# Layer 2's forward x transform on rows folded onto their mirror image

## The chip, the cores and the metric

The kernel runs on one core of a Trainium2 chip. The metric is the device time of one execution in microseconds, as the median of several runs. The engines are TensorE (PE, with its weight loads shown as PEld), VectorE (DVE), ScalarE (ACT), GpSimd (POOL), and the DMA queues of SyncE (SP) and POOL.

## The reference

Four layers are applied to x of shape (16, 16, 256, 256) in float32: samples, channels, rows y, columns x. Each normalizes x over groups of two channels, computes something from it and adds that to x. Layer 0 is a 3x3 convolution written with FFTs, layer 1 a diagonal 5-tap convolution, layer 3 a quantized 3x3 convolution. The change touches layer 2 alone:

```python
x = x + _L2_conv_ref(_gn(x), ty, tx, weights_pole1, weights_pole2, weights_residue)

alpha = jnp.fft.fft2(x, axes=(-2, -1))
A = 1.0 / (omega1[:, None, None, None] - weights_pole1[None])
Bm = 1.0 / (omega2[:, None, None, None] - weights_pole2[None])
S = jnp.einsum('ikpq,oikp,xikq->oxik', weights_residue, A, Bm)
output_residue1 = jnp.einsum('biox,oxik->bkox', alpha, S)
C = jnp.einsum('biox,oikp->bikpx', alpha, A)
D = jnp.einsum('bikpx,xikq->bikpq', C, Bm)
output_residue2 = jnp.einsum('bikpq,ikpq->bkpq', D, weights_residue)
x1 = jnp.fft.ifft2(output_residue1, s=(Ny, Nx), axes=(-2, -1)).real
...
return x1 + x2 / Nx / Ny
```

`alpha` is the two-dimensional Fourier transform of each image. `S` mixes channels at each frequency, and `x1` is the inverse transform of the mixed spectrum. `C` and `D` reduce alpha over both frequencies against the poles' responses; they give `x2`.

## The kernel before

The program has five stages, one after the other: layers 0 and 1 (their last matmul starts at 1271 us), the forward transforms of layer 2 (`forth` from 1342 to 2147 us), the mixing of channels at each frequency (to 2920 us), the inverse transforms (2958 to 3806 us), and layer 3 (from 3833 us). The change is in the second stage, in tables that it reads, and in one table of the inverse transform (`last`).

Transforms are matmuls with tables of cosines and sines. The input is real, so only 129 of 256 frequencies in x are kept, `fx`: 128 first, then the even ones (65 columns with 128), then the odd ones (64 columns).

The work of the second stage is ordered by the list `order`: for each block of four samples, for each pair of channels, for each of the four samples. One entry of it is a call of `quarters` (line 763), which prepares the two images of a pair; there are 128. `quarters` loads the images with y on the partitions (`xt`), adds and subtracts the upper and the lower half of y (`u`: the sum with the mean folded in by VectorE at line 768, the difference by GpSimd at line 769), and from `u` makes sums and differences of column w and column w + 128 (`qd`, two operations of VectorE, line 772). The sums carry the even x frequencies, the differences the odd ones. Everything that goes through the helper `tt` has line 191 in the profile.

For each image then come:

- `forth` (from line 775): the transform along y. For each of the two column parities c, `v` (that is `qd`) is the weight matrix of 128 x 128, and the y tables (line 782) and `hats[0]`, the y poles' responses (line 785), stream through, 128 columns each. ScalarE scales the result into `y` (line 787): its partitions are the 128 columns w, its columns 128 real parts, 128 imaginary parts, 128 for the poles.
- `across` (from line 790): the transform along x. `y`'s real and imaginary parts are the weights, in turn; the tables `x1` and `x2` stream through (line 796), 2 x 65 columns for the even frequencies and 2 x 64 for the odd ones, all over 128 rows. ScalarE copies the first part's sums out of PSUM (`pc`, line 801), and two operations of VectorE combine both parts into `al`, for the frequencies fy and -fy (lines 803 and 804). After four samples `al` goes to DRAM in two DMAs, one on SP's queue and one on POOL's (line 807).
- `onto` (from line 810): after four images, the poles' part of `y` is multiplied with `hats[1]`, the x poles' responses, in four parts of the array of 32 columns (line 817). VectorE multiplies the result with the residues (`prod`), GpSimd adds the products up (`acc`).

The order on TensorE is written out by hand: `forth` of one image, then `across` of the image before it, then, once in four images, `onto`. The order on the other engines is a scheduler's, and it is fixed in the program. Between these steps `transforms` and `prepared` work out further tables for this stage and for the next (`hat`, `qe`, `qg`, `qw`, `ps_t`, `af`, `l`).

Buffers: `xt` four, `u` and `qd` three each, `ps_y` three PSUM banks, `ps_a` three (an image takes two), `ps_d` two.

Of the kernel before, what the change touches and what calls it, by code (L numbers as in the profile page):

```python
# [57 lines left out]
P = 128  # L58
C = 16
# [12 lines left out]
def constants():  # L72

    n = np.arange(N)
    m = np.arange(128)
    even, odd = 2 * np.arange(64), 2 * np.arange(64) + 1
    fx = np.concatenate([[128], even, odd])
    fy = np.stack([np.concatenate([even, odd]), -np.concatenate([[128], even[1:], odd])], 1).reshape(-1)

    def cos(a, b):  # L80
        return np.cos(2.0 * np.pi * (np.outer(a, b) % N) / N)

    def sin(a, b):
        return np.sin(2.0 * np.pi * (np.outer(a, b) % N) / N)


    y1 = [np.concatenate([cos(m, even), cos(m, [128]), -sin(m, even[1:])], 1),
          np.concatenate([cos(m, odd), -sin(m, odd)], 1)]
    by_fx = [fx[:65], fx[65:]]
    x1 = [np.concatenate([cos(m, f), -sin(m, f)], 1) for f in by_fx]  # L90
    x2 = [np.concatenate([sin(m, f), cos(m, f)], 1) for f in by_fx]

    full = np.stack([np.stack([cos(o, m), sin(o, m)], 1) for o in (n[0::2], n[1::2])], 1)


    inv = np.stack([np.stack([np.concatenate([cos(even, m), v * cos([128], m), v * sin(even[1:], m)], 0),
                              np.concatenate([cos(odd, m), v * sin(odd, m)], 0)], 1) for v in (-1, 1)], 2)

    h = 0.5 / N**2
    last = np.stack([h * np.concatenate([cos([0], m), 2 * cos(even[1:], m), cos([128], m), -2 * sin(even[1:], m)], 0),  # L100
                     h * np.concatenate([2 * cos(odd, m), -2 * sin(odd, m)], 0)], 1)
    p = np.arange(P)[:, None]
    q = np.arange(P)[None, :]
    c16, c8, c4 = np.arange(C)[None, :], np.arange(8)[None, :], np.arange(S)[None, :]
    s = p % S
    strip = np.stack([s == c4, s + 1 == c4, s - 1 == c4], 1)
    nat = (n + 128) % N - 128


    f4 = p % 4  # L110
    alone = np.concatenate([np.where(f4 < 2, 0.5, 1.0), np.where(f4 < 2, 0.5 - f4, 1.0)], 1)
    im = p // 32 % 2 == 1
    sa = np.where(p < 64, [[1.0, 1.0]], [[1.0, -1.0]])
    sb = np.where(p < 64, [[1.0, -1.0]], [[-1.0, -1.0]])
    parts = {
        "y1": np.concatenate(y1, 1), "x1": np.concatenate(x1, 1), "x2": np.concatenate(x2, 1),
        "full": full, "inv": inv, "last": last, "alone": alone,
        "not0": 1.0 * (p > 0),
        "strip": strip,
        "chan": p % 64 // S == c16,  # L120
        "imag": 1.0 * (p // C % 2 == 1), "real": 1.0 * (p // C % 2 == 0),
        "group4": (p % 32 // 4 == q % 32 // 4) / 16.0,
        "first": p == 4 * c8,
        "mod": p % 8 == c8,


        "turn": np.stack([np.where(p < 64, 1.0, -1.0), np.where(p // 32 % 2 == 0, -1.0, 1.0),
                          1.0 * (p // 32 % 2 == 1), 1.0 * (p // 32 % 2 == 0)], 1),

        "turn_q": np.concatenate([np.where(im, sb, -sa), np.where(im, -sa, -sb)], 1),  # L130
        "vi": 1.0 * ((p // 64 == np.arange(16)[None, :] // 8) & (p % 8 == np.arange(16)[None, :] % 8)),
        "diag": p // NP % 4 == c4,
        "own": p // 32 == c4,
        "m1": np.diag(np.where(p[:, 0] // 16 % 2 == 0, 1.0, -1.0)) / (2 * N) ** 2,
        "m2": (p == q + 16 - q // 16 % 2 * 32) / (2 * N) ** 2,
        "eye": 1.0 * (p == q),
        "mean": np.full((P, P), 1.0 / P),
        "ones": np.ones((P, P)),
        "quarter": np.concatenate([np.where(p // 16 % 2 == 0, 0.25, 0.0), np.where(p < 64, 0.25, 0.0)], 1),
        "sign": np.where(p < 64, 1.0, -1.0),  # L140
        "nat": nat.reshape(128, 2),
    }
    at, where, cols = 0, {}, []
    for k, v in parts.items():
        v = np.asarray(v, np.float32).reshape(P, -1)
        where[k] = (at, v.shape[1])
        at += v.shape[1]
        cols.append(v)
    fxs = np.where(fx == 128, -128, fx)
    rows = np.concatenate([fy, np.where(fy == -128, 128, fy), fxs, fx])  # L150
    return np.concatenate(cols, 1), rows.astype(np.float32)[None, :], where
# [14 lines left out]
def layers(ctx, tc, x, w0, w1, w3, sw, bias, ty, tx, p1a, p1b, p1c, p2a, p2b, p2c, resa, resb,  # L166
# [402 lines left out]
    def sums_over_q(pool, psum):  # L569
# [32 lines left out]
        for h in range(HC):  # L602
            for k0 in range(0, C, KQ):
# [14 lines left out]
                       bc(bc(vi[:, v], 1, 8), 1, 2 * KQ), MUL)  # L618
                yield
                for k in range(KQ):  # L620
                    ps = psum.tile([P, 512], F32, tag="ps_a", name="ps_t")
                    for m in range(2):
                        nc.tensor.matmul(ps[:, m * NX : (m + 1) * NX], start=m == 0, stop=m == 1, rhs=e[:, k],
                                         lhsT=w[:, 2 * k + m].rearrange("p v r i -> p (v r i)"), skip_group_check=True)
                    nc.scalar.copy(t2[:, h, k0 + k].rearrange("p r x -> p (r x)"), ps[:, 0 : 2 * NX])
                    if k % 2:
                        yield

        a = new(pool, [HC, C], "qa")
        Q.tensor_copy(a, t2[:, :, :, 0, 0])  # L630
        Q.tensor_scalar(t2[:, :, :, 0, 0], t2[:, :, :, 1, 0], -1.0, None, MUL)
        Q.tensor_copy(t2[:, :, :, 1, 0], a)
        yield

    afs, lss, sks = {}, {}, {}
    KC = 4
# [40 lines left out]
    with ExitStack() as es:  # L677
        wp = es.enter_context(tc.tile_pool(name="b_w", bufs=1))
        ps_y = es.enter_context(tc.tile_pool(name="b_ps_y", bufs=3, space=PSUM))
        ps_a = es.enter_context(tc.tile_pool(name="b_ps_a", bufs=3, space=PSUM))  # L680
        ps_d = es.enter_context(tc.tile_pool(name="b_ps_d", bufs=2, space=PSUM))

        y1 = table(wp, "y1").rearrange("p (a f) -> p a f", a=2)
        x1, x2 = table(wp, "x1"), table(wp, "x2")
# [9 lines left out]
        ap_ = es.enter_context(tc.tile_pool(name="b_a", bufs=3))  # L694
        with ExitStack() as tmp:
            tp = tmp.enter_context(tc.tile_pool(name="b_t", bufs=1))
            full = table(wp, "full").rearrange("p (h m f) -> p h m f", m=2, h=2)
            nat, diag = table(tp, "nat"), table(tp, "diag")
            ws = []
            for m, t in enumerate((ty, tx)):  # L700
# [6 lines left out]
            def transforms(m, i0, ni, pool):  # L707
# [22 lines left out]
                for o in range(2):  # L730
                    for i in range(0, ni, nb):
                        cols = slice(i * KP, (i + nb) * KP)
                        for r, parts_ in enumerate(((re, im), (im, nre))):
                            ps = ps_y.tile([P, 8, KP], F32, tag="ps_y", name="ps_hat")
                            to = ps[:, 0:nb]
                            for k, v_ in enumerate(parts_):
                                nc.tensor.matmul(to.rearrange("p i k -> p (i k)"), lhsT=full[:, o, k],
                                                 rhs=v_[:, o, cols], start=k == 0, stop=k == 1)
                            hat = hats[m][:, o, i0 + i : i0 + i + nb]
                            if m:  # L740
                                nc.scalar.copy(hat.rearrange("p i (r k) -> p i r k", r=2)[:, :, r], to)
                            else:
                                nc.scalar.copy(hat.rearrange("p i (t r k) -> p i t r k", t=4, r=2)[:, :, :, r],
                                               to.rearrange("p i (t k) -> p i t k", t=4))
# [18 lines left out]
        def quarters(b, g):  # L763
# [3 lines left out]
            u = up.tile([P, 2, 2, N], F32, tag="u", name="u")  # L767
            V.scalar_tensor_tensor(u[:, 0], xt[:, :, 0, :], bc2[:, b, g, 1:2], xt[:, :, 1, :], ADD, ADD)
            tt(Q, u[:, 1], xt[:, :, 0, :], xt[:, :, 1, :], SUB)
            qd = up.tile([P, 2, 2, 2, P], F32, tag="qd", name="qd")  # L770
            for c, op_ in enumerate((ADD, SUB)):
                tt(V, qd[:, c], u[:, :, :, 0:P], u[:, :, :, P:N], op_)
            return qd

        def forth(b, i, v):

# [12 lines left out]

        def across(b, i, y, al):  # L790

            sums = []
            for part, f in ((0, x1), (1, x2)):
                ps = ps_a.tile([P, 512], F32, tag="ps_a", name="ps_a")
                for c, (lo, hi) in enumerate(((0, 65), (65, NX))):
                    nc.tensor.matmul(ps[:, 0 : 2 * NX].rearrange("p (r x) -> p r x", r=2)[:, :, lo:hi],
                                     lhsT=y[:, c, part * P : (part + 1) * P], start=c == 0, stop=c == 1,
                                     rhs=f[:, 2 * lo : 2 * hi].rearrange("p (r x) -> p r x", r=2))
                sums.append(ps[:, 0 : 2 * NX])
            pc = ap_.tile([P, 2 * NX], F32, tag="pc", name="pc")  # L800
            nc.scalar.copy(pc, sums[0])
            flat = lambda t: t.rearrange("p r x -> p (r x)")
            V.scalar_tensor_tensor(flat(al[:, 0, :, :, b % BG]), sums[1], not0, pc, MUL, ADD)
            V.scalar_tensor_tensor(flat(al[:, 1, :, :, b % BG]), pc, not0, sums[1], MUL, SUB)
            if b % BG == BG - 1:
                for s_, eng in enumerate((nc.sync, Q)):
                    eng.dma_start(rows2[:, s_, :, i // 8, i % 8, b // BG, :],
# [653 lines left out]
```

## Time and profile before

| | |
|---|---|
| median of 3 runs | 4229.16 us (4228.94 to 4233.02) |
| the profiled execution's own time | 4226.85 us |
| its span, first to last instruction | 4225.1 us |
| mean granted TensorE clock | 0.956 of full speed |

Busy time over the span:

| engine | us | share | instructions |
|---|---|---|---|
| PE | 3663.5 | 87% | 55904 |
| PEld (weight loads, beside PE) | 2807.8 | 66% | 55904 |
| DVE | 2986.8 | 71% | 5347 |
| ACT | 2573.9 | 61% | 3643 |
| POOL | 1886.8 | 45% | 3099 |

The costliest groups of the stage that the change touches:

| line, engine, operation | count | busy us | mean ns of one |
|---|---|---|---|
| L782 PE matmul `ps_y` from the y tables | 2048 | 321.5 | 280 |
| L785 PE matmul `ps_y` from `hat` | 2048 | 314.5 | 276 |
| L787 ACT `y` from `ps_y` | 512 | 296.0 | 581 |
| L191 DVE `qd` from `u` (within 1342 to 2147 us) | 250 | 185.0 | 778 |
| L803 DVE `al` (same) | 254 | 173.3 | 682 |
| L804 DVE `al` (same) | 254 | 169.2 | 666 |
| L191 POOL `u` from `xt` (same) | 122 | 157.9 | 1294 |
| L768 DVE `u` from `xt` (same) | 122 | 126.2 | 1036 |

How to read it: a row of the profile names line, engine, operation and tiles (output, then inputs, without buffer numbers), the count, the busy time, the mean length of one, and the idle time of the engine just before it with what ended it. A float32 matmul leaves two records on PE, and each has its weight load on PEld. Records of matmuls overlap, since each is shown from its start to the modelled end of its pipeline; the rate is read from the distance between starts. Idle time of an engine that is not the bottleneck costs nothing.

### The profile page before, as it was taken

The page shows a single profiled execution, that of the slowest core. Times are in us where ns is not written, and L with a number is a line of the kernel's source. Part 1 is how long each engine was busy: PE and PEld are TensorE (multiplying, and loading weights), DVE is VectorE, ACT ScalarE, POOL GpSimd, SP SyncE. Part 2 cuts the span into 40 slices and gives each one's busy share as a digit, 9 for nine tenths or more (in the row PEclk, how much of TensorE's full clock was granted, in tenths as well). Part 3 has the DMA queues.
Part 4 walks back from the last instruction along what each step waited for, and adds up shares of the span by engine and source line. Part 5 has one row for each costly group of instructions (what it writes and reads, how often), then busy time and mean ns, then how long its engine had stood idle before and what let it go on. Part 6 is the DMA issues. An engine that isn't in the chain of part 4 may idle for free. (4 is left out here: it accounts for less than half of the span.)

```text
span 4225.1 us, 131595 instructions
## 1 busy us (share of the span) xinstructions
PE 3663.5 (87%) x55904; PEld 2807.8 (66%) x55904; DVE 2986.8 (71%) x5347; ACT 2573.9 (61%) x3643; POOL 1886.8 (45%) x3099
## 2 busy tenths in 40 slices
PE   4999999999985999999976777675999999996777
PEld 1455555555554999999965555564888888883444
DVE  4676767667668878887865565554677777768988
ACT  2867677686743544444456666666444544447998
POOL 2233242332433434443356565663666666662222
PEclk9999999999997999999999999997999999998998
DMA  6767677576734555455536666667878888877998
GB/s 137 173 152 191 156 176 180 144 195 147 181 81 120 173 162 172 160 167 167 181 118 180 191 183 187 183 184 196 227 222 234 234 237 240 242 209 279 349 350 314
DMA packets 479643, 821.10 MB, mean 194 GB/s; under 512 B 39696, under 2 KB 371472, under 8 KB 463632
## 3 DMA queue, kind: packets, MB, share of 16 engines
q1 hardware_dynamic: 431952, 644.63, 53.8%
q0 software_dynamic: 47104, 168.06, 13.3%
q8 instruction: 440, 7.21, 0.7%
q14 instruction: 147, 1.20, 0.1%
HBM read 408.84 MB, written 336.07 MB: 176 GB/s over the span
## 5 line engine op out<-in xcount | busy, mean ns | idle before, releaser
L383 PE MATMUL ps<-va,wt 128*64 128x512 f32 (+1 forms) x1632 | 670.2, 572 | 11.4 <-POOL va L355 9.2
L383 PE MATMUL ps<-vb,wt 128*64 128x512 f32 (+1 forms) x1632 | 668.4, 571 | 4.7 <-DMA vb<-va 4.7
L787 ACT ACTIVATE y<-ps_y,bc 128x384 f32<-128x384 f32 x512 | 296.0, 581 | 348.2 <-PE ps_y L785 347.7
L404 ACT ACTIVATE v<-xt,nm 32x2048 f32<-32x2048 f32 x248 | 497.2, 2005 | 9.8 <-PE ps L418 3.5
L1004 PE MATMUL ps_m<-z,sk 128*32 128x64 f32 x16384 | 341.9, 229 | 183.6 <-issue 142.9
L418 PE MATMUL ps<-v,w1s 128*64 128x259 f32 x4096 | 480.1, 394 | 11.0 <-DVE v L402 6.7
L1004 PEld LDWEIGHTS ps_m<-z,sk 128*32 128x32 f32 x16384 | 309.3, 115 | 233.2 <-issue 162.5
L191 POOL TENSOR_TENSOR w<-rq 128x512 f32<-128x512 f32 x256 | 334.4, 1328 | 262.5 <-ACT rq L1147 261.8
L383 PEld LDWEIGHTS ps<-va,wt 128*64 128x64 f32 x1632 | 223.4, 138 | 311.3 <-issue 283.0
L418 PEld LDWEIGHTS ps<-v,w1s 128*64 128x64 f32 x4096 | 335.9, 141 | 132.7 <-issue 22.3
L1146 PE MATMUL ps_o<-exp,fs 128*128 128x128 f32 x2048 | 400.8, 278 | 10.9 <-ACT fs L1194 10.8
L1145 PE MATMUL ps_o<-c_last,zt 128*128 128x128 f32 x2048 | 399.3, 277 | 0.0
L191 DVE TENSOR_TENSOR ob<-ps_m,other 128x256 f32<-128x256 f32 x512 | 193.2, 419 | 287.3 <-ACT other L1030 273.3
L1291 PE MATMUL ps_c<-q,wt 64*64 64x512 bf16 (+1 forms) x4608 | 292.0, 404 | 101.7 <-ACT o L1338 84.4
L1145 PEld LDWEIGHTS ps_o<-c_last,zt 128*128 128x128 f32 x2048 | 324.3, 194 | 60.8 <-issue 60.8
L925 PE MATMUL ps_s<-t,l 128*32 128x258 f32 x4096 | 316.0, 402 | 39.1 <-issue 21.5
L191 POOL TENSOR_TENSOR u<-xt 128x512 f32<-128x512 f32 x128 | 167.2, 1306 | 389.0 <-DVE qd L191 280.8
L1146 PEld LDWEIGHTS ps_o<-exp,fs 128*128 128x128 f32 x2048 | 314.6, 194 | 12.8 <-ACT fs L1194 12.8
L782 PE MATMUL ps_y<-c_y,qd 128*128 128x128 f32 x2048 | 321.5, 280 | 1.1 <-ACT y L787 0.9
L1291 PEld LDWEIGHTS <-wt 64*64 64x64 bf16 x4800 | 181.0, 114 | 212.9 <-issue 145.6
L785 PE MATMUL ps_y<-hat,qd 128*128 128x128 f32 x2048 | 314.5, 276 | 0.0
L1147 ACT COPY rq<-ps_o 128x512 f32<-128x512 f32 x256 | 150.0, 587 | 262.4 <-PE ps_o L1146 260.8
(235 smaller groups left out, 8509.2 us busy)
## 6 DMA issues: line engine op xcount, KB each, us to landing
xt<-x2d SPq DMA_DIRECT2D x256, 512.0 KB, 4.3
z<-alphad SPq DMA_DIRECT2D x258, 258.0 KB, 4.1
xt<-in_x_dram SPq DMA_DIRECT2D x256, 256.0 KB, 7.7
x2d<-x2s POOLq DMA_DIRECT2D x256, 256.0 KB, 5.0
mixd<-ob SPq DMA_DIRECT2D x256, 256.0 KB, 4.6
ot<-mixd SPq DMA_DIRECT2D x256, 256.0 KB, 6.3
x3d<-xt SPq DMA_DIRECT2D x128, 512.0 KB, 5.3
xt<-x3d SPq DMA_DIRECT2D x64, 1024.0 KB, 8.9
```

What stands on the lines that cost most here:

```text
L191: eng.tensor_tensor(o, a, b, op)
L383: nc.tensor.matmul(ps[halves[h], lo:hi, :], lhsT=wt0[:, w, :], rhs=v[:, 2 * t + lo : 2 * t + hi, j : j + N], start=j == 0 and k == 0, stop ...
L404: nc.scalar.activation(to, o.xt[c][q_], AF.Identity, bias=o.g.nm[q_, 1:2])
L418: nc.tensor.matmul(ps[halves[h], k, 0:U], lhsT=o.w1[:, w : w + 64], rhs=v1[:, lo : lo + U], start=first_, stop=not first_)
L782: nc.tensor.matmul(to[:, :, a, :], lhsT=v[:, c, a, i % 2, :], start=a == 0, stop=a == 1, rhs=y1[:, a].rearrange("p (r f) -> p r f", r=2))
L785: nc.tensor.matmul(ps[:, 2 * P : 3 * P], lhsT=v[:, c, a, i % 2, :], start=False, stop=a == 1, rhs=hats[0][:, a, i], skip_group_check=True)
L787: nc.scalar.activation(y[:, c, :], ps[:, 0 : 3 * P], AF.Copy, scale=bc2[:, b, i // 2, 0:1])
L925: nc.tensor.matmul(ps[at : at + 32, d, 0 : 2 * NX], lhsT=ls[h][:, k + d - k0, n], rhs=t2[:, h, k + d].rearrange("p r x -> p (r x)"), start ...
L1004: nc.tensor.matmul(to, lhsT=sk[:, x_], rhs=z[:, :, x_], start=True, stop=True)
L1145: nc.tensor.matmul(ps[:, a, c, :], lhsT=zts[d][:, a, c, :], rhs=last[:, c, :], start=True, stop=False)
L1146: nc.tensor.matmul(ps[:, a, c, :], lhsT=fs[:, d, a, :], rhs=ey[:, d, c, :], start=False, stop=True)
L1291: nc.tensor.matmul(o, lhsT=wt[half[h], w, :], rhs=src, start=i == 0, stop=i == len(work[0]) - 1)
```

## The change

After `qd` is made, each of its rows of 128 columns is folded once more: column m (0 to 63) is added to and subtracted from its mirror image, column 127 - m. The mirror lies about half a sample, so the tables take angles of pi (2m + 1) f / 256 (`cos_`, `sin_`). With this phase, the real part of a frequency comes from the 64 sums alone (with cosines) and the imaginary part from the 64 differences alone (with sines). For this `qd`'s second half is made in another order of its quarters. The fold is two operations of GpSimd, and its result goes back into the buffer of `u`; `quarters` returns that. After `forth` the partitions 0 to 63 of `y` hold the sums and 64 to 127 the differences.

`across` now issues eight matmuls for an image where it issued four. Each has 64 rows, 128 columns of weights and 65 or 64 streamed columns; those on partitions 0 to 63 write one PSUM bank, those on 64 to 127 another. `x1` and `x2` have 129 columns each instead of 258. The phase stays in `alpha`; the last table of the inverse transform (`last`) takes it out, the x poles' responses are made with a table of their own (`fold`), and an exchange of real and imaginary parts at frequency 128 in `prepared` is no longer needed. `ps_a` has two buffers of two banks instead of three of one, `ps_d` one instead of two, `qd` two instead of three.

```diff
+    def cos_(a, b):
+        return np.cos(np.pi * (np.outer(a, 2 * b + 1) % (2 * N)) / N)
+    def sin_(a, b):
+        return np.sin(np.pi * (np.outer(a, 2 * b + 1) % (2 * N)) / N)
...
-    by_fx = [fx[:65], fx[65:]]
-    x1 = [np.concatenate([cos(m, f), -sin(m, f)], 1) for f in by_fx]
-    x2 = [np.concatenate([sin(m, f), cos(m, f)], 1) for f in by_fx]
+    m64 = np.arange(64)
+    x1, x2 = (np.concatenate([cos_(fx, m64).T, v * sin_(fx, m64).T], 0) for v in (-1, 1))
...
+    there, back = full[..., :64], full[..., :63:-1]
+    v = np.array([1, -1])[None, :, None, None]
+    fold = np.concatenate([there + v * back, there - v * back], 3) / 2
...
-                    ps = psum.tile([P, 512], F32, tag="ps_a", name="ps_t")
+                    ps = psum.tile([P, 2, 512], F32, tag="ps_a", name="ps_t")[:, 0]
...
-        a = new(pool, [HC, C], "qa")
-        Q.tensor_copy(a, t2[:, :, :, 0, 0])
-        Q.tensor_scalar(t2[:, :, :, 0, 0], t2[:, :, :, 1, 0], -1.0, None, MUL)
-        Q.tensor_copy(t2[:, :, :, 1, 0], a)
...
-        ps_a = es.enter_context(tc.tile_pool(name="b_ps_a", bufs=3, space=PSUM))
-        ps_d = es.enter_context(tc.tile_pool(name="b_ps_d", bufs=2, space=PSUM))
+        ps_a = es.enter_context(tc.tile_pool(name="b_ps_a", bufs=2, space=PSUM))
+        ps_d = es.enter_context(tc.tile_pool(name="b_ps_d", bufs=1, space=PSUM))
...
-            qd = up.tile([P, 2, 2, 2, P], F32, tag="qd", name="qd")
-            for c, op_ in enumerate((ADD, SUB)):
-                tt(V, qd[:, c], u[:, :, :, 0:P], u[:, :, :, P:N], op_)
-            return qd
+            qd = up.tile([P, 2, 4, P], F32, tag="qd", name="qd", bufs=2)
+            w4 = u.rearrange("p h c (q w) -> p (h c) q w", q=4)
+            tt(V, qd[:, 0].rearrange("p j (q w) -> p j q w", q=2), w4[:, :, 0:2], w4[:, :, 2:4], ADD)
+            tt(V, qd[:, 1].rearrange("p j (q w) -> p j q w", q=2), w4[:, :, 0::3], w4[:, :, 2:0:-1], SUB)
+            v = u.rearrange("p h c w -> p (h c w)").rearrange("p (j w) -> p j w", w=P)
+            from_ = qd.rearrange("p c j w -> p (c j) w")
+            for h, op_ in enumerate((ADD, SUB)):
+                tt(Q, v[:, :, 64 * h : 64 * h + 64], from_[:, :, 0:64], from_[:, :, :63:-1], op_)
+            return v.rearrange("p (c a i) w -> p c a i w", c=2, a=2)
...
-            sums = []
-            for part, f in ((0, x1), (1, x2)):
-                ps = ps_a.tile([P, 512], F32, tag="ps_a", name="ps_a")
-                for c, (lo, hi) in enumerate(((0, 65), (65, NX))):
-                    nc.tensor.matmul(ps[:, 0 : 2 * NX].rearrange("p (r x) -> p r x", r=2)[:, :, lo:hi],
-                                     lhsT=y[:, c, part * P : (part + 1) * P], start=c == 0, stop=c == 1,
-                                     rhs=f[:, 2 * lo : 2 * hi].rearrange("p (r x) -> p r x", r=2))
-                sums.append(ps[:, 0 : 2 * NX])
-            pc = ap_.tile([P, 2 * NX], F32, tag="pc", name="pc")
-            nc.scalar.copy(pc, sums[0])
+            ps = ps_a.tile([P, 2, 512], F32, tag="ps_a", name="ps_a")
+            work = [(part, f, c, lo, hi) for part, f in ((0, x1), (1, x2)) for c, (lo, hi) in enumerate(((0, 65), (65, NX)))]
+            for n, (part, f, c, lo, hi) in enumerate(work):
+                for h in range(2):
+                    at = slice(64 * h, 64 * h + 64)
+                    nc.tensor.matmul(ps[:, h, part * NX + lo : part * NX + hi], lhsT=y[at, c, part * P : (part + 1) * P],
+                                     rhs=f[at, lo:hi], start=n == 0, stop=n == 3, skip_group_check=True)
+            even, odd = ps[:, :, 0:NX], ps[:, ::-1, NX : 2 * NX]
+            pc = ap_.tile([P, 2, NX], F32, tag="pc", name="pc")
+            nc.scalar.copy(pc, even)
...
+            V.scalar_tensor_tensor(al[:, 0, :, :, b % BG], odd, not0, pc, MUL, ADD)
+            V.scalar_tensor_tensor(al[:, 1, :, :, b % BG], pc, not0, odd, MUL, SUB)
```

## The prediction

> **What bounds the kernel now.** I read the page first (TensorE busy 87% of the span), then the stretches, to find the stage that the diff touches: the loop of layer 2 over `forth` and `across`, from the first `forth` matmul at 1342 us to the last at 2147 us. This line sums it (columns: length, busy us and instructions of PE, PEld, DVE, ACT, POOL, then granted clock, DMA share, GB/s).
>
> ```profile
> 1342.00:2147.00 805.00, 783.43 (x10369) 767.86 (x10368) 654.36 (x1022) 392.58 (x839) 312.01 (x299) 0.99 0.50 162
> ```
>
> TensorE is busy 97% of 805 us, DVE 81%, POOL 39%, DMA half. The waits in this stage say that the others follow TensorE:
>
> ```profile
> ACT y L787 <- PE ps_y L785: 347.7, 477, 4.6
> POOL u L191 <- DVE qd L191: 280.8, 90, 8.7
> PE ps_a L796 <- DVE al L804: 11.6, 7, 2.5
> ```
>
> TensorE waited 11.6 us for `al`, its longest such row. So the stage takes 805/256 = 3.14 us for one (sample, channel), 6.29 us for a pair (one call of `quarters`). Third, the timeline of the middle of the stage:
>
> ```profile
> 1701.37 1.29 DVE L191 TENSOR_TENSOR qd<-u 128x512 f32<-128x512 f32 x2 [0.61 <-PE ps_y L785]
> ...
> 1702.80 1.28 POOL L191 TENSOR_TENSOR u<-xt 128x512 f32<-128x512 f32 x1 [4.14 <-issue]
> ...
> 1703.61 1.02 DVE L768 SCALAR_TENSOR_TENSOR u<-xt,bc 128x512 f32<-128x512 f32 x1
> ...
> 1703.78 1.06 PE L796 MATMUL ps_a<-c_x,y 128*128 128x130 f32 x8
> ...
> 1704.77 0.76 PE L817 MATMUL ps_d<-hat,y 128*32 128x32 f32 x64
> ...
> 1705.46 0.71 PE L782 MATMUL ps_y<-c_y,qd 128*128 128x128 f32 x4
> ...
> 1707.19 1.88 POOL L191 TENSOR_TENSOR acc<-acc,prod 128x256 f32<-128x256 f32 x2
> ...
> 1707.62 2.00 DVE L191 TENSOR_TENSOR qd<-u 128x512 f32<-128x512 f32 x2 [0.90 <-PE ps_y L785]
> ```
>
> Two things are to be seen. (a) DVE operations with both inputs in SBUF do not run beside a POOL operation. The two `qd` take 1.29 us alone and 2.00 us beside `acc`; `u` of L768 starts at 1703.61, POOL ends at 1704.08, and DVE ends 0.55 us after that. In the single records the two engines alternate: acc to 1707.93, qd to 1708.49, acc to 1709.07, qd to 1709.62. Over the stage `qd` has a median of 0.685 us where POOL is idle and 1.18 us where POOL covers over half of it; `al`, with one input in PSUM, has 0.685 and 0.686. (b) A change of the shape of the array costs TensorE: L796 has eight records 0.113 us apart, so its turn ends at 1704.68, L817 starts 0.09 us later; L817's sixteen rounds of 31.5 ns end at 1705.27, L782 starts 0.19 us later.
>
> **Part 1, the matmuls of `across`.** Before: four matmuls per (sample, channel), two records each (a weight load and a stream), 8 x 0.113 = 0.90 us. After: eight matmuls with 64 rows and 65 or 64 columns, sixteen records in two halves of the array. The streams halve, but each half still loads `y` as 128 columns of weights. What a load costs without a stream to hide it is shown by a matmul of six columns:
>
> ```profile
> 159.00 0.39 PE L291 MATMUL ps_gn<-mv,c_group 128*128 128x6 f32 x2
> ...
> L291 PE MATMUL ps_gn<-mv,c_group x38: 254/275/379, 31.6 to 1279.3; 128*128 128x6 f32 x38
> ```
>
> Two records end within 0.39 us, one takes 0.275: the second comes 0.11 us after the first, as in L782 with 128 columns (0.112). So the load alone sets 0.11 us. No row shows 64-row parts in f32. Bounds: loads of the two halves side by side, 8 x 0.11 = 0.88 us (a change of -0.02); in turn, 16 x 0.11 = 1.76 us (+0.86); side by side and at half the time, 0.44 us (-0.46). I take the first: L817 loads four 32-column parts in a round of 31.5 ns, while 128 columns in one load take 110, so loads into different parts do run side by side there. Changes of shape: two per group of four units now, nine after (into and out of each `across`, one more at `onto`): 7/4 x 0.09 to 0.19 = 0.16 to 0.33 us per unit, or 0 if row parts need none. TensorE: 3.14 - 0.02 + (0 to 0.33) = 3.12 to 3.45 us, a stage of 799 to 883 us (in turn: 1024 to 1108). It gains nothing.
>
> The Trainium skill speaks on both sides here. "TensorEngine Tiling (Array Packing)", Theoretical Speedup, gives up to 2x for a contraction of 64 rows or fewer; by it TensorE would save 0.45 us x 256 = 115 us. "TensorE: Matmul & The Clock Gate", LDWEIGHTS (loading the stationary operand), says that a load's time follows its columns and not its rows; by it the saving is nil. The row of L291 speaks for the second, though it has 128 rows.
>
> **Part 2, the fold on POOL.** Each pair gets two more POOL operations of 512 elements, and they stand between `qd` and the matmuls. In the order of the changed program POOL does, for 123 of 128 pairs, subtract S (`u` second half), fold F1, fold F2, and only then S of the next pair. DVE does U (L768), Q1, two `al`, Q2, two `al`; both folds wait for Q2. In 110 of 128 pairs the two `al` stand between Q1 and Q2 (in 119 of 128 nothing did before). So S, Q1, Q2, F1, F2 become one chain, and the next pair's chain begins where this one ends:
>
> S 1.28, hand-over 0.07 (an event record stands that far ahead of the `qd` it releases), Q1 0.61 (start to start), Q2 0.69, hand-over 0.07, F1 1.27, U 0.55, F2 1.27: 5.81 us. U belongs there by (a): it comes up on DVE while POOL holds the port, is let in between two POOL operations, and delays the next by its 0.55. The pair of `al` between Q1 and Q2 adds 1.03 (L803 starts at 1709.55, what follows the pair at 1710.58). The fold's price is not in the trace (rows of 64, one input read backwards). Nearest rows: POOL additions of 512 elements take 1.04 (`qg`), 1.26 at least (`w`, `o`) and 1.78 (`o` beside DVE). I take 1.27, as S and `w` also read two separate stretches.
>
> Work that POOL has between F2 and the next S: 26 DMA issues x 0.73, 26 `acc` x 0.72, 12 `qw` x 1.07, 10 `af` x 0.73, 7 `l` x 0.62, 8 others 6.7 in all: 69 us. What stands between S and F1 (36 DMA issues, 30 `acc`) is hidden behind Q1 and Q2. On DVE, eight reciprocals of 3.38 us (L610) outlast the 2.8 us that DVE has free during F1, F2 and S by some 0.6 each: 5 us. The five early S save 5 x 1.28 = 6 us.
>
> Stage: 128 x 5.81 + 110 x 1.03 + 69 + 5 - 6 = 925 us, or 7.2 us per pair against 6.2 to 6.9 for TensorE. The chain wins, TensorE waits for it, and `al` is not late (DVE's `al` lag two pairs behind the fold). 925 - 805 = +120 us.
>
> The "GPSIMD Engine Reference", Performance pitfalls for Q7 kernels, adds half for reads whose step is over 8 bytes; the backward step is 4 bytes, so by it the fold costs no more, and past that cliff the sum would be 128 x 1.27 us = 163 us higher. No row here has a backward read.
>
> **Part 3, the rest at nothing.** The pools `ps_a` (three single banks to two double ones) and `ps_d` (two to one) change who waits: a unit used two of three `ps_a`, now one of two, which is looser; `ps_d` is next written some four units after its last write, and its readers are two `prod` of 0.41 us. If a DVE delay undid that cover, each of 64 groups would cost TensorE at most 0.8 us, 51 us in all, while it idles anyway. ACT's `pc` stays 258 elements (0.37 us). The `qa` copies leave (0.7 + 0.4 + 0.2 us, off the path). The extra table is loaded ahead of the stage.
>
> **Sum.** 4226.85 (this execution; span 4225.1) + 120 = 4347; the median shown is 2.3 us above it, so 4349.
>
> **Rivals.** (1) Loads of the halves in turn: TensorE sets 1024 to 1108 us, time 4448 to 4532. For it: records issue in order. Against: L817. (2) The backward read is slow: F at 1.78 adds 2 x 0.51 x 128 = 131 us, 4480; in part, 4400 and up. For it: no such row. (3) The chain stays shorter than TensorE: F at 1.04 and U in a gap leave 5.81 - 0.46 - 0.55 = 4.80, a stage of 614 + 113 + 68 = 795 us; TensorE's 799 to 883 decide, 4223 to 4307. For it: 281 us of POOL waiting in the old stage; against: the alternation seen in (a). (4) Faster: as (3), with loads at half the time (TensorE 2.7 to 3.0 us a unit, at most 771 us) and half of POOL's 69 us hidden: 760 us, 4184. It decides once a pair takes under 6.2 us on both engines; for it only the halved streams speak, against it L291.
>
> **How the numbers follow.** About 0.2% (8.5 us) is what a measurement of this kernel tells from no change. Chances: forecast (4300 to 4400) 0.58; rival 1 0.10; rival 2 0.12; rival 3 0.11, of which 0.04 within 0.2%; rival 4 0.09. Faster 0.09, same 0.04, slower 0.87. The range 4250 to 4465 leaves out rival 4, the lower half of rival 3 and most of rival 1 (under 0.2).
>
> **What would show it.** The stage lengthens to about 925 us and PE's share in it falls below 90%; the chain of POOL `u<-xt`, DVE `qd`, POOL `u<-qd` shows as waits of PE on POOL; POOL is over 75% busy there; the fold's mean lies at 1.3 to 1.8 us with DVE's U between the two; records of `across` stand 0.055 us apart (two halves in 0.11). It is wrong if PE stays over 95% busy, if those records stand 0.11 apart (rival 1) or 0.03 (rival 4), or if F alone takes much over 1.3.

## The result, and the profile after

| | median | lowest to highest | runs |
|---|---|---|---|
| before | 4230.98 us | 4228.94 to 4233.02 | 4 |
| after | 4430.65 us | 4424.57 to 4440.96 | 4 |

The ratio is 1.0474, with a 95% interval from 1.0451 to 1.0498: 200 us slower. The profiled execution of the changed kernel is the one of 4440.96 us (span 4439.2), 214 us above the profiled one of before. The stage from the first to the last `forth` matmul takes 1008 us (1346 to 2354) where it took 804; that is 204 of the 214.

The stretch of that stage in the profile after, with the columns as before (length, busy us and instructions of PE, PEld, DVE, ACT, POOL, then granted clock, DMA share, GB/s):

```profile
1346.00:2355.00 1009.00, 900.10 (x12399) 837.71 (x12397) 710.77 (x1015) 417.76 (x838) 643.14 (x549) 0.94 0.39 130
```

TensorE's busy share falls from 97% to 89%, POOL's rises from 39% to 64%, and no engine is busy throughout, which points to a chain of operations that wait for each other; the experiments below test it. The waits in the same stretch (total us, times, longest) say which chain:

```profile
POOL u L199 <- DVE qd L199: 211.6, 86, 4.6
DVE qd L199 <- POOL u L199: 208.4, 98, 5.5
...
PE ps_a L804 <- DVE al L810: 64.9, 40, 5.7
...
PE ps_g L847 <- DVE pt L199: 14.5, 2, 7.7
```

POOL waits for VectorE's `qd` as long as VectorE waits for POOL's `u`: the two hand the work to and fro. TensorE's own longest row is `al`, 64.9 us where it was 11.6. The costliest groups of the page have the new operations:

```profile
L199 POOL TENSOR_TENSOR u<-qd 128x512 f32<-128x512 f32 x256 | 352.6, 1399 | 218.6 <-DVE qd L199 213.0
...
L804 PE MATMUL ps_a<-c_x,y 64*128 64x65 f32 (+1 forms) x4096 | 294.3, 285 | 64.9 <-DVE al L810 64.9
L199 DVE TENSOR_TENSOR qd<-u 128x512 f32<-128x512 f32 x256 | 197.5, 776 | 209.9 <-POOL u L199 208.4
```

The fold (`u<-qd` on POOL) takes 1.40 us in the mean; its median over the single records is 1.277 and its least 1.253. The timeline of a pair late in the stage shows how TensorE comes to wait:

```profile
2249.68 2.39 DVE L770 SCALAR_TENSOR_TENSOR u<-xt,bc 128x512 f32<-128x512 f32 x1
...
2252.62 1.26 POOL L199 TENSOR_TENSOR u<-xt 128x512 f32<-128x512 f32 x1
...
2253.17 0.61 PE L792 MATMUL ps_y<-hat,u 128*128 128x128 f32 x4
...
2253.91 1.20 DVE L199 TENSOR_TENSOR qd<-u 128x512 f32<-128x512 f32 x1 [1.84 <-POOL u L199]
2255.03 0.66 DVE L809 SCALAR_TENSOR_TENSOR al<-ps_a,c_not,pc 128x258 f32<-128x258 f32 x1
2255.54 0.65 DVE L810 SCALAR_TENSOR_TENSOR al<-pc,c_not,ps_a 128x258 f32<-128x258 f32 x1
2256.02 0.68 DVE L199 TENSOR_TENSOR qd<-u 128x512 f32<-128x512 f32 x1
2256.24 0.86 PEld L804 LDWEIGHTS ps_a<-c_x,y 64*128 64x128 f32 x14 [2.65 <-DVE al L810]
2256.24 1.00 PE L804 MATMUL ps_a<-c_x,y 64*128 64x65 f32 x14 [2.46 <-DVE al L810]
...
2256.85 1.28 POOL L199 TENSOR_TENSOR u<-qd 128x512 f32<-128x512 f32 x1 [2.29 <-DVE qd L199]
```

POOL ends the subtraction S at 2253.88; VectorE's Q1 (the first `qd`) has stood at the head of its queue for it for 1.84 us, and behind Q1 stands an `al` whose inputs were there long before. TensorE waits for that `al`, since `across` needs its PSUM buffer. POOL then waits 2.29 us for Q2 before it can fold.

In what follows, "the pace" is the distance between the first `forth` matmuls of successive pairs in the trace, as a mean over pairs 100 to 124: behind the last block border, and with no further tables being worked out. It is 5.81 us before and 7.09 us after.

### The profile page after: what moved, and what is told of

The parts are those of the page before. It is cut to its first block, busy times and chain, and to the rows that moved or that the text cites. A ratio compares the mean times of both kernels' runs of the same rounds, so it can differ in the third digit from the quotient of the medians.

```text
span 4439.2 us, 135957 instructions
## 1 busy us (share of the span) xinstructions
PE 3765.1 (85%) x57952; PEld 2865.5 (65%) x57952; DVE 3044.2 (69%) x5347; ACT 2598.1 (59%) x3643; POOL 2219.3 (50%) x3352
## 5 line engine op out<-in xcount | busy, mean ns | idle before, releaser
L199 POOL TENSOR_TENSOR u<-qd 128x512 f32<-128x512 f32 x256 | 352.6, 1399 | 218.6 <-DVE qd L199 213.0
L789 PE MATMUL ps_y<-c_y,u 128*128 128x128 f32 x2048 | 354.8, 298 | 11.0 <-ACT hat L743 7.0
L804 PE MATMUL ps_a<-c_x,y 64*128 64x65 f32 (+1 forms) x4096 | 294.3, 285 | 64.9 <-DVE al L810 64.9
L199 DVE TENSOR_TENSOR qd<-u 128x512 f32<-128x512 f32 x256 | 197.5, 776 | 209.9 <-POOL u L199 208.4
L792 PE MATMUL ps_y<-hat,u 128*128 128x128 f32 x2048 | 327.3, 285 | 0.0
L804 PEld LDWEIGHTS ps_a<-c_x,y 64*128 64x128 f32 x4096 | 258.4, 194 | 99.7 <-DVE al L810 72.9
```

The lines of the kernel that those rows point to most:

```text
L199: eng.tensor_tensor(o, a, b, op)
L789: nc.tensor.matmul(to[:, :, a, :], lhsT=v[:, c, a, i % 2, :], start=a == 0, stop=a == 1, rhs=y1[:, a].rearrange("p (r f) -> p r f", r=2))
L792: nc.tensor.matmul(ps[:, 2 * P : 3 * P], lhsT=v[:, c, a, i % 2, :], start=False, stop=a == 1, rhs=hats[0][:, a, i], skip_group_check=True)
L804: nc.tensor.matmul(ps[:, h, part * NX + lo : part * NX + hi], lhsT=y[at, c, part * P : (part + 1) * P], rhs=f[at, lo:hi], start=n == 0, st ...
```

## The experiments

| run | time (its own before) | ratio [95%] | stage us | pace us |
|---|---|---|---|---|
| before | | | 804 | 5.81 |
| after | 4430.65 (4230.98) | 1.0474 [1.0451, 1.0498] | 1008 | 7.09 |
| no fold | 4318.75 (4229.93) | 1.0203 [1.0183, 1.0223] | 886 | 6.39 |
| fold, old `across` | 4404.99 (4229.93) | 1.0411 [1.0392, 1.0430] | 974 | 7.10 |
| third fold | 4599.58 (4229.93) | 1.0856 [1.0822, 1.0889] | 1164 | 8.48 |
| order ahead | 4395.45 (4229.93) | 1.0385 [1.0360, 1.0410] | 967 | 6.39 |
| fold on VectorE | 4372.68 (4239.50) | 1.0315 [1.0293, 1.0337] | 944 | 6.56 |
| before, tables out | 4321.36 (4239.50) | 1.0198 [1.0169, 1.0228] | 755 | 5.81 |
| after, tables out | 4487.42 (4239.50) | 1.0593 [1.0561, 1.0624] | 932 | 7.04 |
| before, new buffers | 4255.22 (4239.50) | 1.0039 [1.0024, 1.0055] | 821 | 5.81 |
| no fold, double stream | 4338.66 (4240.90) | 1.0233 [1.0218, 1.0249] | 904 | 6.39 |
| no fold, two `across` | 4287.10 (4240.90) | 1.0110 [1.0088, 1.0131] | 853 | 6.05 |
| order ahead, tables out | 4409.69 (4240.90) | 1.0393 [1.0373, 1.0413] | 845 | 6.39 |
| before, `project` later | 4217.45 (4236.72) | 0.9955 [0.9938, 0.9973] | 790 | 5.81 |

### Each half of the change alone

Without the fold, `quarters` returns `qd`, so TensorE's work is all of the new and POOL's all of the old:

```diff
-            for h, op_ in enumerate((ADD, SUB)):
-                tt(Q, v[:, :, 64 * h : 64 * h + 64], from_[:, :, 0:64], from_[:, :, :63:-1], op_)
-            return v.rearrange("p (c a i) w -> p c a i w", c=2, a=2)
+            return from_.rearrange("p (c a i) w -> p c a i w", c=2, a=2)
```

> The changed kernel without the two fold operations: forth takes qd as it is, so layer 2's transform is not the reference's; all matmuls stay. Chain theory (S, Q1, al, Q2, F1, F2 on GpSimd and VectorE set the period of a pair): without F the chain is gone, TensorE sets the stage with 3.14 + 0.18 us per image (the changes of the array's shape), 846 us of stage, about 4270 us (4255 to 4300). TensorE theory (the 64-row matmuls and their loads set the stage): nothing moves, 4400 to 4440. Half and half: about 4350.

The other half is the kernel before with the new `quarters`, its folds included, and the old `across` with its old PSUM buffers.

> The kernel before with the new quarters alone (new qd, fold on GpSimd), and across as before on 128 rows, with the buffers of before; the tables do not fit the fold, so layer 2's transform is not the reference's. Chain theory: the period is the chain's, 7.1 us in a quiet pair and 7.9 on average as in the changed kernel, 4400 to 4435 us. TensorE theory: TensorE is as before, 4225 to 4245. Buffers (one ps_d, two ps_a) as the cause of the part beyond the forecast: 4350.

In the third run the second of the two folds is issued twice:

```diff
-            for h, op_ in enumerate((ADD, SUB)):
+            for h, op_ in ((0, ADD), (1, SUB), (1, SUB)):
```

> The changed kernel with the second fold operation issued twice (same result): one more GpSimd operation of 1.27 us in each of 128 pairs. Chain theory: all of it is on the path, +150 to +165 us, 4580 to 4600. TensorE theory: hidden, 4425 to 4445. If only part of the pairs is bound by the chain, in between.

Without the fold the time is 4318.75, 19 us above what the expectation allowed if the chain was the cause. The stretch of that stage:

```profile
1341.00:2228.00 887.00, 861.55 (x12396) 803.30 (x12396) 720.16 (x1014) 418.39 (x838) 326.57 (x297) 0.98 0.44 147
```

TensorE is busy 97% of it: the new `across` is dearer for TensorE by itself, by 0.58 us a pair. The expectation had counted 0.18 us an image for the changes of shape where they take 0.29 (below), which is 28 us of the 40 by which the stage is longer than the 846 expected; the run also has the new buffers, which cost the kernel before 16 us (below). The old `across` behind the fold gives 4404.99, at the pace of the changed kernel. So the two costs do not add up, 89 and 175 us against 200: where no tables are worked out they are two bounds, TensorE at 6.39 and the chain at 7.1 us, and the later one decides. The 25 us between 175 and 200 lie in the pairs with tables and at the block borders, since the pace is the same; `across` and its buffers were both the old ones in that run, so it does not tell which of them costs that. A third fold adds 169 us to the changed kernel (162 by the ratios), 1.26 to 1.32 us a pair: what it takes on POOL, with next to nothing of it hidden. This is what a chain does, and not what an engine with 36% of its time free would do.

### Is it the chain's order, or the port?

First, VectorE's and GpSimd's order written out by hand, so that S is done three pairs ahead and `qd` and the folds two pairs ahead (`u` in four buffers):

```diff
...
-            v = quarters(b, i0 // 2)
+            if n + 3 < len(order):
+                us[n + 3] = quarters(order[n + 3][0], order[n + 3][1] // 2)
+            if n + 2 < len(order):
+                vs[n + 2] = folded(us.pop(n + 2))
+            v = vs.pop(n)
```

> The changed kernel, result kept, with the order on VectorE and GpSimd written out by hand in this stage: U and S three pairs ahead, Q1, Q2 next to each other and F1, F2 two pairs ahead, four u buffers. The work is the same, the chain is cut: no operation waits for one of the same pair that was just issued. Chain theory: GpSimd needs about 4.9 us a pair, VectorE 4.6 and its waits for the port, TensorE 6.5 sets the stage, 4260 to 4320 us. Port theory (the two engines exclude each other so often that the order does not matter): 4380 or more. TensorE theory: 4400 to 4440.

The total missed, at 4395.45, but the pace fell to 6.39, exactly that without the fold. The loss is in the pairs beside which tables are worked out: a mean of 8.26 us in pairs 4 to 30, against 7.98 in the changed kernel. A written order takes each table operation in its turn, also where it still waits for another engine; that this is the cause is argued here, and the next runs test where it lies. The tables were taken out of the loop (worked out before and after it), in the kernels before and after, and then in the one with the written order:

```diff
+        for n in (2, 4, 8, 10):
+            transforms(n // 2 % 2 ^ 1, 8 + 4 * (n > 7), 4, None)
         for n, (b, i0) in enumerate(order):
...
-            if n in (2, 4, 8, 10):
-                transforms(n // 2 % 2 ^ 1, 8 + 4 * (n > 7), 4, None)
-            if n > 15 and (n % 2 or n > 60):
-                next(aside, None)
```

> The kernel before, result kept, with the tables for the next stage made after the loop and the rest of this stage's tables made ahead of it, so that the loop holds pairs alone. It is a baseline for the next run: its loop should take 128 x 5.88 us = 753 us and the block borders; the time as a whole rises by the work that now stands alone, by some 30 to 120 us. No theory says more of it alone.

> The changed kernel with the same move. Theory: the part beyond the forecast (200 measured, 119 forecast) is what the table work costs in this stage now that GpSimd and VectorE have no pairs ahead; then the loop takes 128 x 7.14 us and three block borders, some 930 us, and the kernel stands 165 to 180 us above the baseline of the run before this. Rival (the chain itself is longer than summed and the table work innocent): 195 us or more above the baseline.

> The changed kernel with VectorE's and GpSimd's order written out (the subtraction three pairs ahead, `qd` and fold two pairs ahead), as in the earlier run with that order, and with the further tables worked out before and after the loop, as in the earlier run of the changed kernel without them (4487.4 us, its loop 932.8 us). If the chain of S, Q1, Q2, F1, F2 held that loop back through its order alone, the loop falls to TensorE's pace of 6.37 us a pair: 128 x 6.37 = 815 us and some 15 for the block borders, 830 us, and the time to 4487 - 103 = 4384 us. If it is the port (the busy time of VectorE and GpSimd together), the order changes nothing: 4487 us, and at most 20 less.

Without tables the changed kernel stands 166 us above the kernel before without tables (4487.42 against 4321.36), at the lower end of the 165 to 180 expected (its rival asked for 195 or more), and its loop takes 932 us where some 930 were expected.

The stretches of the loop, first of the changed kernel without tables, then of the one with the written order as well:

```profile
1383.00:2316.00 933.00, 854.62 (x12207) 798.09 (x12205) 632.44 (x970) 392.06 (x766) 600.26 (x504) 0.95 0.42 140
```

```profile
1378.00:2223.00 845.00, 827.64 (x12202) 776.03 (x12203) 688.96 (x971) 392.56 (x765) 604.22 (x500) 0.98 0.46 155
```

The written order, with the fourth `u` buffer that it needs, takes 88 us from the loop, at the same work on POOL (600 and 604 us), and TensorE is again busy 98% of it; the pace is 6.39 in every stretch between two block borders. The buffer was not tried by itself; GpSimd waited for a free `u` (for the matmuls that read it) for 23 us in all in the loop without the written order, so those waits are not the 88 us. The port (VectorE's two-input operations and POOL's shutting each other out) is a share of the chain's length and not a bound of its own here. The time fell by 78 us (4487 to 4410; 85 by the ratios), not by the 103 expected; 845 against 830 is the block borders, at 14.1 to 14.7 us where the pace is 6.39.

The pair of runs without tables also prices them. They cost the loop 49 us before (804 to 755) and 76 after (1008 to 932).

The fold on VectorE instead (`tt(V, ...)` for `tt(Q, ...)`):

> The changed kernel, result kept, with the two fold operations on VectorE (0.61 us each by the rate of qd) instead of GpSimd. Chain theory with the port: GpSimd is back to one operation of a pair that reads SBUF, the chain is S 1.3, Q1 0.6, al 1.0, Q2 0.6, F1 0.6, F2 0.6 = 4.8 us and VectorE needs about 5.9 us a pair, under the 6.4 us that TensorE needs without a fold: about the time of the run without a fold, 4319, up to 4350 us. If VectorE's work in itself sets the stage (al late for TensorE): 4380 or more. If it is the fold's place in the chain and not its length: no gain, 4400 to 4430.

```profile
1342.00:2287.00 945.00, 878.35 (x12393) 817.07 (x12392) 846.07 (x1262) 417.82 (x840) 325.10 (x296) 0.97 0.42 140
```

The two folds no longer stand on POOL and the time falls by 58 us (67 by the ratios), to 4372.68, between the values that the expectation gave for its theories. VectorE is now busy 90% (846 of 945 us), but that alone does not hold TensorE up: behind the last block border VectorE is busy 90% as well, TensorE is busy 98%, and the pace is 6.56, near TensorE's 6.39. Most of the 58 us by which this stage is longer than the one without a fold (944 against 886) lies in the pairs beside which tables are worked out, 24 us of it in the first 32 pairs. Why they take longer was not tested.

### What TensorE pays for the new `across`

With the fold left out, two runs. In one, six of the eight matmuls stream their table twice behind one load of weights:

```diff
...
-                                     rhs=f[at, lo:hi], start=n == 0, stop=n == 3, skip_group_check=True)
...
+                                     rhs=bc(f[at, lo:hi], 1, 2) if k == 2 else f[at, lo:hi],
+                                     start=n == 0, stop=n == 3, skip_group_check=True)
```

> The fold is left out (so the transform is not the reference's), and in six of the eight matmuls of `across` the table streams twice behind one load of `y`, the second copy into columns of PSUM that nothing reads (130 or 128 columns per record where there were 65 or 64). It is compared with the kernel without the fold, 4318.8 us, in which TensorE sets the pace. If the loads of `y` set the time of the new `across` (two halves side by side, 0.11 us for 128 columns), the longer stream hides behind the loads: 4319 us, 10 either way. If the streams set it, twelve of sixteen records per image take 0.027 us longer: 0.32 us x 256 = 83 us, 4400 us.

In the other, `across` is issued for both images of a pair together:

```diff
...
-                if before:
+                for before in pending if k == 0 else ():
                     ended()
...
```

> The fold is left out, and `across` of the two images of a pair is issued in one piece, so the array changes its shape two times per pair fewer. If each change costs TensorE 0.09 us, the kernel without the fold (4318.8 us) becomes 2 x 0.09 x 128 = 23 us faster: 4296 us, between 4285 and 4305. If a change of shape costs nothing, or the waits for PSUM that the longer piece brings take the gain, it stays at 4319 us or becomes slower.

The same group of matmuls in the profile without the fold, and in that with the doubled stream (busy us, mean ns, idle before):

```profile
L802 PE MATMUL ps_a<-c_x,y 64*128 64x65 f32 (+1 forms) x4096 | 286.4, 280 | 4.9 <-DVE al L808 4.9
```

```profile
L807 PE MATMUL ps_a<-c_x,y 64*128 64x130 f32 (+2 forms) x4096 | 287.4, 278 | 15.9 <-DVE al L814 15.9
```

Twice the columns take the same time on TensorE, and the pace stays at 6.39; of the 83 us that the streams would have cost, 13 are seen (0.3%), and TensorE's waits for `al` are 11 us longer. So the streams do not set the time of `across`. The loads of `y` do: their records come in twos, one for each half, every 0.112 us, as often as one load of 128 rows does in `forth`. Halving the streams could not gain anything here.

Issuing two `across` together gains 39 us by the ratios (0.93%), 0.34 us a pair, more than the 23 expected. The distances between records tell why: into a turn of `across` (TensorE changes from the whole array, in `forth`, to its row halves) 205 ns where `forth` runs at 112, then 154 for the second pair of records where the later ones stand at 105; out of it 202, and the second record of the next `forth` at 213. That is 0.093 + 0.049 in and 0.09 + 0.101 out, 0.33 us for a turn; the expectation counted 0.09 each way and left out the second records. One turn per pair less is 0.33 us, as measured.

### The buffers, and the block borders

The kernel before with the changed buffers alone (`ps_a` two of two banks, `ps_d` one, `qd` two):

```diff
-        ps_a = es.enter_context(tc.tile_pool(name="b_ps_a", bufs=3, space=PSUM))
-        ps_d = es.enter_context(tc.tile_pool(name="b_ps_d", bufs=2, space=PSUM))
+        ps_a = es.enter_context(tc.tile_pool(name="b_ps_a", bufs=2, space=PSUM))
+        ps_d = es.enter_context(tc.tile_pool(name="b_ps_d", bufs=1, space=PSUM))
...
```

> The kernel before, result kept, with the changed kernel's buffers alone: one ps_d, two ps_a of two banks, two qd. Chain theory: nothing, 4225 to 4250 us. Buffer theory (project and onto wait for the single ps_d, the waits of 7.6 us ahead of project's matmul): 4250 to 4290.

It costs 16 us where TensorE sets the pace, all in the pairs with tables and at the borders; the pace is the same. In the changed kernel this part was not taken out by itself.

At the three borders between blocks of four samples a pair takes 16.7, 18.6 and 16.8 us in the changed kernel (12.5, 12.1 and 9.5 before). TensorE's timeline at the second of them:

```profile
1867.36 0.61 PE L792 MATMUL ps_y<-hat,u 128*128 128x128 f32 x4
1874.73 0.77 PE L847 MATMUL ps_g<-pt,c_m 128*128 128x128 f32 x2 [6.76 <-DVE pt L199]
1875.45 0.80 PE L847 MATMUL ps_g<-qt,c_m 128*128 128x128 f32 x2
1876.17 1.97 PE L804 MATMUL ps_a<-c_x,y 64*128 64x65 f32 x16
```

The matmuls of `project` need the last `acc`, which stands on POOL behind two folds, a DMA issue and S, and all of TensorE's queue stands behind them. The last run issues `project` two images later, in the kernel before:

```diff
-                if due:
+                if due and b % BG + k > 1:
                     project(*due)
```

> The kernel before, with the matmuls of `project` (once per block of four samples) issued two images later. In the kernel before, TensorE waits 16.1 us for `pt` and 2.0 us for `qt` ahead of them, in three places; in the changed kernel it waits there too, and the forecast has no term for it. If these waits stand on the path that sets the end, the time falls by 12 to 18 us, to 4223 to 4229 us beside a kernel before at 4241. If the wait only moves (VectorE's or GpSimd's queue is late anyway), it stays within 4 us of the kernel before.

TensorE at the first border, by the row of the kernel before and then by the rows of this run:

```profile
1555.42 0.80 PE L841 MATMUL ps_g<-pt,c_m 128*128 128x128 f32 x2 [3.77 <-DVE pt L191]
```

```profile
1555.67 0.61 PE L785 MATMUL ps_y<-hat,qd 128*128 128x128 f32 x4
1556.12 0.39 PE L841 MATMUL ps_g<-pt,c_m 128*128 128x128 f32 x2
1556.34 0.39 PE L841 MATMUL ps_g<-qt,c_m 128*128 128x128 f32 x2
1556.56 1.06 PE L796 MATMUL ps_a<-c_x,y 128*128 128x130 f32 x8
```

The wait is gone, a border pair takes 6.3 to 7.1 us, and the kernel is faster than the one before: 4217.45 us, 0.45% (0.27 to 0.62) or 19 us below its own before. (The 16.1 us in the expectation adds the waits of the weight loads to those of the matmuls; TensorE's own in the stage are 8.4.) The stage is 14 us shorter, more than the wait. The clock accounts for most of the rest: the stage has 6.8 us at half speed instead of 17.1, which is 5 us of work; see the end. The same edit in the changed kernel was not tried.

## Why the prediction was right, and where it fell short

The direction, the mechanism and the range held (4250 to 4465); the value, 4349, was 82 us too low. The measured 4431 also lies outside 4300 to 4400, which had a chance of 0.58; "4400 and up" stood there for a slow backward read, and the fold is not slow. So the range held by its width, and with terms missing from the sum. By its steps:

- **The chain.** Right in links and size. Forecast 6.84 us a pair with the `al` in it, and 0.30 for POOL's DMA issues and `acc`: 7.14. The pace is 7.09, and in four successive pairs POOL's first folds stand 6.68, 7.05, 8.24 and 6.68 us apart, 7.16 in the mean. The links follow each other in the trace: in pairs 100 to 124, by medians, S 1.26, Q1 0.69, the pair of `al` 0.92, Q2 0.69, 0.15 until F1, F1 1.28, and S directly behind F2. U does come between: in 23 of these 24 pairs F2, S or Q1 is some 0.45 to 0.5 us longer than alone (the forecast had 0.55 in every pair). Writing the order out removes the chain and leaves 6.39.
- **How TensorE feels it.** The statement that "`al` is not late" was wrong. No row of TensorE's waits names POOL's fold; it waits for `al`, which stands behind Q1 in VectorE's queue while Q1 waits for S. The size of the chain does not depend on this, but the sign to look for does.
- **The loads.** Right. Records of the two halves come 7 and 105 ns apart in turn, two loads within 0.11 us, and twice the stream costs next to nothing. Of the two rules that were weighed, the gain of up to 2x of "TensorEngine Tiling (Array Packing)", Theoretical Speedup, does not appear in these matmuls, and that of "TensorE: Matmul & The Clock Gate", LDWEIGHTS (loading the stationary operand), agrees: 64 rows of 128 columns load no faster than 128 rows. (In the row of L291, from which this was read, the second matmul starts 0.133 us after the first; 0.11 is the distance between their ends, and 0.108 that between the starts of their loads.)
- **Changes of shape.** Forecast 0.16 to 0.33 us per image, measured 0.29 (half of 6.39 less 5.81). That this fits is partly luck. The 0.19 was read from an end of L817's turn at 1705.27, but its last record starts at 1705.339 and L782's first follows 0.126 us later; what makes up for it, the late second records, was not in the sum.
- **The fold's price.** Forecast 1.27, median 1.277, as much as the subtraction S, which reads forwards (median 1.28 in the kernel before). This agrees with "GPSIMD Engine Reference", Performance pitfalls for Q7 kernels, which adds half only for steps over 8 bytes; it does not speak of backward reads.
- **POOL over 75% busy** was a wrong sign: 64%. POOL itself stands some 2.1 to 2.5 us in most pairs waiting for Q1, `al` and Q2, which the forecast's own chain implied.
- **The term that failed is the work beside the chain.** The sum took 36 us for the tables (31 of POOL's own operations, 5 of the reciprocals) and nothing for the block borders. The tables cost 76. Part of the difference shows as waits: ahead of table operations POOL stands 24.6 us in the stage, 14.5 for VectorE, 5.5 for TensorE and 4.4 for a DMA, and holds S and the folds back with it; and VectorE is busy 78 us longer with the tables than without (711 and 632), of which the sum counted 5. How the 40 us divide among these was not separated. The borders take 16.8, 16.8 and 15.9 us in the run without tables, three times some 9.5 us over the pace, and about 30 with the pairs next to them. The remaining 13 of the 83 us (1008 less 925) are spread over the loop; in the run without tables the `al` stand between Q1 and Q2 in 121 pairs and not in 110, which is 11 us at 1.03 each.
- **The buffers at nothing.** Wrong where TensorE is the bound (16 us); what they cost beside the chain is open.

Of the rivals, loads in turn (1), the slow backward read (2) and loads at half the time (4) are out by the records above. Rival 3, TensorE alone deciding, is what the kernel without the fold shows: 4318.75, against 4223 to 4307 worked out for it. With the fold it did not come about: F takes 1.28 and not 1.04 us, and U is not hidden.

## What to carry to other kernels

Once two in-order engines that hand work to and fro set the pace, an operation put between them costs its full length (here the third fold), however idle its engine is: sum the chain from one pass to the next, and see whether the next pass can begin before this one ends. Work that is strewn into such a loop can cost more than its own time (here 76 us where 36 were counted), so price it from a run with that work taken out. A matmul that waits for another engine's last result is better issued a few independent matmuls later in the queue, as `project` shows in the kernel before.

## What the runs showed of the hardware

TensorE's clock fell after short waits. In the changed kernel, around the wait of 2.46 us shown above (the third number from the right is the granted clock):

```profile
2235.00:2252.00 17.00, 16.50 (x234) 15.38 (x233) 12.21 (x19) 7.81 (x17) 12.35 (x11) 1.00 0.43 147
2252.00:2256.20 4.20, 1.78 (x16) 1.59 (x15) 2.36 (x5) 1.43 (x3) 2.56 (x3) 1.00 0.79 252
2256.20:2261.00 4.80, 4.76 (x34) 4.55 (x35) 2.47 (x4) 0.96 (x3) 4.15 (x3) 0.64 0.23 82
2261.00:2264.00 3.00, 3.00 (x92) 2.89 (x93) 2.94 (x6) 1.13 (x3) 0.50 (x2) 1.00 0.52 157
```

The clock is full up to the wait, at 0.64 in the mean of the 4.8 us after it, and full again. By the clock's own records, which show 0.50 and 1.00 alone, the stage has 126 us at half speed after and 17 before.

The length of a wait alone does not decide. In the kernel before, a wait of 2.01 us at one border brought 0.50 soon after, while one of 2.00 us at another and one of 2.48 us (from 1813.1 us) left the clock at 1.00. The stretch behind the wait of 2.01 us, then those around the wait of 2.48 us:

```profile
1760.00:1762.00 2.00, 2.00 (x11) 2.00 (x11) 2.00 (x6) 0.38 (x1) 0.72 (x1) 0.50 0.61 233
```

```profile
1812.00:1814.00 2.00, 1.10 (x10) 0.91 (x9) 2.00 (x1) 1.25 (x3) 0.00 (x0) 1.00 0.00 0
1814.00:1816.00 2.00, 0.41 (x3) 0.41 (x4) 2.00 (x5) 0.00 (x0) 0.00 (x0) 1.00 0.00 0
1816.00:1818.00 2.00, 2.00 (x76) 1.84 (x75) 2.00 (x5) 0.00 (x0) 0.75 (x1) 1.00 0.54 203
```

The records suggest what does. All stretches at half speed begin on one grid of 3.41 us within a run and last whole steps of it. In the kernel before, the four full-speed steps ahead of them held 2.28 to 3.35 us of TensorE's idle time, and no other full-speed step held over 1.64; the waits of 2.00 and 2.48 us fall across the border of two steps. In the changed kernel the two groups overlap (1.17 to 3.41 us ahead of half speed, up to 1.77 elsewhere), so no sharp limit comes out. "TensorE: Matmul & The Clock Gate", The HAM clock gate, lets the clock fall after an idle window of about 3.4 us; here less idle time than that was enough.

So a wait of TensorE can cost more than its length where TensorE then sets the pace, as with `project` (14 us of stage for 8.4 us of waits). How much of the changed kernel's 200 us this is was not separated; at full speed half of the 126 and of the 17 us would be left, so it is at most 55, and the chain hides part of that.

A turn from the whole array to its row halves and back costs 0.33 us in these runs. "TensorEngine Tiling (Array Packing)", Key Properties, says that changing the mode drains TensorE, without a time.
